# A planned graph-network kernel: own due times for every step, loads planned as a queue, a column of ones, split projections, and biases moved into ScalarE

## The chip, the cores and the metric

The kernel runs on one core of one Trainium2 chip. The metric is the device time of one execution in microseconds (us), the lower the better. The program that is launched is timed whole; the trace covers the span of its instructions.

## What is computed

Two layers run over 128 graphs (`B`) of 128 nodes, with 64 features per node. Both end in a residual sum and a layer norm.

```
mask = adj > 0
h    = relu((x @ W1a)[:, :, None] + (x[:, :, None] - x[:, None]) @ W1b + b1)   # 192 wide, per edge
hm   = einsum('bjkh,bjk->bjh', h, mask)
x1   = layernorm(x + hm @ W2 + deg * b2)
agg  = einsum('bmn,bnd->bmd', adj, x1)
h1   = elu(agg @ V1 + c1);  h2 = elu(h1 @ V2 + c2)                             # 128 wide
out  = layernorm(x1 + h2 @ V3 + c3)
```

About 6% of the entries of `mask` are one, so the kernel does not build all 128 x 128 edges of a graph: it sorts the nodes by degree, gives each sorted node a fixed number of edge slots (`BLOCKS`, 7 to 22), and handles only those 1323 slots per graph. A dense version stands behind a branch for graphs that do not fit; in the profiled execution it does not run.

## The kernel before

Graphs go in 64 pairs; the two graphs of a pair share the partitions where their data is 64 wide. One **round** is the work on one pair's worth of every step, though the steps of one round belong to different pairs: pair `p` is prepared some rounds before its edges are handled and finished some rounds after.

Each step is a Python generator that yields work items `(engine, cost, what it waits for, PSUM banks, function)`:

- `prepare` counts degrees (L511, VectorE), makes sort keys (L518-519, GpSimd), spreads them over the partitions (L524) together with a row of positions (L526, TensorE), ranks the nodes (L533) and makes a permutation matrix (L541, VectorE) that reads the row of positions from PSUM.
- `sort_x` and `project_a` sort `x` (L556) and compute the node term (L570 on TensorE, L577 on ScalarE adds `b1`); GpSimd and VectorE compute a correction for the unused slots (L584, L596, L603).
- `sort_mask` sorts the mask (L612, L615), forms prefix sums (L626) and nine one-hot tables (L636, VectorE).
- `turn` transposes the adjacency and `x` (L651, L652); `project_c` computes the neighbour term in float32 (L669), adds `b2` to its last 64 columns (L672) and splits it in three bfloat16 parts (L679, L683, L686, L688).
- `unit` is run nine times per pair, on four PSUM banks in turn: ScalarE writes the node term into a bank (L811), TensorE adds the gathered neighbour term with 18 matmuls in 64-column tiles (L823), VectorE sums absolute values over the slots (L832).
- `finish` subtracts the correction (L741), multiplies by `W2` (L746), adds the part from `project_c` (L750), counts degrees with two one-column matmuls against `mtp` (L753), undoes the sort (L763), normalizes (`norm`, L696 to L719), and runs layer 1: L770, hidden 1 (a bias row times ones, L778, then L780), `elu`, hidden 2 (a bias row times ones, L786, then L787), `elu`, last (L792, L794), `norm`, store.

In `elu`, the PSUM bank already holds z + 1 (the bias row carries c + 1): ScalarE takes exp(z) with a constant bias of -1 (L729), and VectorE takes max(z + 1, min(exp(z), 1)) (L732), reading one operand from PSUM and one from SBUF. The result is elu(z) + 1; the ones are taken out of the next layer's bias.

`Flow` sets the order of the work. It holds a clock per engine from the written costs, and at each turn takes, among the items that could start within `NEAR` (`NEAR_PE` for TensorE) of the earliest one on that engine, the one with the lowest due time. A change between 64-column tiles (`"PE:t"`) and the full array costs `SWITCH` and adds `HOLD` to the rank. `"PORT"` is a resource that a VectorE and a GpSimd item can both claim. Due times come from one formula: `ROUND * (p - AHEAD) + STEP * step`, with every later item of a thread `STEP` after the one before. The result is a fixed order of instructions on each engine; on the chip only semaphores hold it together, and the costs and the PORT play no part.

All loads are issued by SyncE. At the start, SyncE issues the loads of three pairs with `b1` and `b2` between them, then all constants of layer 1 (`arrive_late`), then the loads of later pairs (`load`, L498, L500). The planner assumes that a load lands 2.5 us after the engines' clock.

## Time and profile before

| what | value |
|---|---|
| median of 3 runs | 788.52 us (788.28 to 788.82) |
| profiled execution | 789.11 us, of which the trace's span is 787.3 us |
| TensorE matmul busy | 756.4 us, 96% of the span |
| VectorE busy | 736.8 us, 94% |
| ScalarE busy | 661.6 us, 84% |
| GpSimd busy | 441.7 us, 56% |
| mean granted TensorE clock | 0.991 |
| first edge unit on TensorE | 32.87 us after the span's start |
| last edge unit's matmuls begin | 763.91 us |

Busy time of an engine counts overlapping instructions once. A matmul's record includes its way through the array, so records of consecutive matmuls overlap; what one of them costs is read from its start to the start of the next. From 110 us on, the order of work repeats each round, and a round lasts 11.49 us.

### The profile page before, as it was taken

The page shows a single profiled execution, that of the slowest core. Times are in us where ns is not written, and L with a number is a line of the kernel's source. Part 1 is how long each engine was busy: PE and PEld are TensorE (multiplying, and loading weights), DVE is VectorE, ACT ScalarE, POOL GpSimd, SP SyncE. Part 2 cuts the span into 40 slices and gives each one's busy share as a digit, 9 for nine tenths or more (in the row PEclk, how much of TensorE's full clock was granted, in tenths as well). Part 3 has the DMA queues.
Part 4 walks back from the last instruction along what each step waited for, and adds up shares of the span by engine and source line. Part 5 has one row for each costly group of instructions (what it writes and reads, how often), then busy time and mean ns, then how long its engine had stood idle before and what let it go on. Part 6 is the DMA issues. An engine that isn't in the chain of part 4 may idle for free.

```text
span 787.3 us, 35836 instructions
## 1 busy us (share of the span) xinstructions
PE 756.4 (96%) x14551; PEld 684.9 (87%) x14552; DVE 736.8 (94%) x2421; ACT 661.6 (84%) x1862; POOL 441.7 (56%) x806
## 2 busy tenths in 40 slices
PE   4889999999999999999999999999999999999994
PEld 2578999999999999999999999999999999999983
DVE  3899999999999999999999999999999999999982
ACT  1868889898989989898998989889898988989862
POOL 4445556555655655565565556556556655655542
PEclk9999999999999999999999999999999999999996
DMA  3000101101101110110111011011101101110000
GB/s 95 2 2 23 27 22 27 30 20 30 26 20 30 27 29 20 30 27 20 30 27 29 21 30 26 20 30 26 30 20 31 26 20 30 27 28 21 9 9 14
DMA packets 63884, 19.91 MB, mean 25 GB/s; under 512 B 46560, under 2 KB 63712, under 8 KB 63712
## 3 DMA queue, kind: packets, MB, share of 16 engines
q1 hardware_dynamic: 63008, 17.25, 9.4%
q8 instruction: 116, 1.90, 1.0%
q14 instruction: 56, 0.46, 0.2%
q10 hardware_dynamic: 704, 0.30, 0.1%
HBM read 13.27 MB, written 4.19 MB: 22 GB/s over the span
## 4 chain that ended last, share of the span: by engine, by line
PE 91%; DVE 4%; ACT 1%; DMA 1%; issue 1%; SPq 1%; POOL 1%; ACTq 0%; POOLq 0%; DVEq 0%
PE e L823 43%; PE m L570 6%; PE m L746 6%; PE m L669 5%; PE m L780 4%; PE m L794 4%; PE m L787 4%; PE m L763 4%; PE m L770 2%; PE m L556 2%; PE m L651 2%; PE m L750 1%; PE m L672 1%; PE m L589 1%; DVE sums L832 1%; DVE oh L636 1%
## 5 line engine op out<-in xcount | busy, mean ns | idle before, releaser
L823 PE MATMUL e<-oh,cp 128*64 128x162 bf16 (+3 forms) x10368 | 376.4, 228 | 5.4 <-ACT e L811 3.8
L823 PEld LDWEIGHTS <-cp 128*64 128x64 bf16 x10368 | 349.1, 110 | 24.4 <-issue 16.9
L832 DVE TENSOR_REDUCE sums<-e 128x54 f32<-128x486 f32 (+8 forms) x576 | 345.6, 610 | 4.2 <-PE e L823 1.9
L811 ACT COPY e<-aj 128x504 f32<-128x504 f32 (+6 forms) x576 | 300.2, 549 | 17.0 <-DVE sums L832 11.6
L636 DVE TENSOR_TENSOR oh<-vp,slotc 128x336 bf16<-128x336 bf16 (+6 forms) x576 | 168.3, 321 | 0.7 <-PE e L823 0.5
L688 POOL TENSOR_TENSOR cp<-r,cp 128x512 bf16<-128x512 f32 x64 | 74.8, 1170 | 73.8 <-ACT cp L686 73.7
L709 POOL TENSOR_TENSOR rs<-ve,mhalf 128x2 f32<-128x2 f32 x128 | 89.2, 697 | 10.6
L577 ACT ACTIVATE aj<-m,b1c 128x128 f32<-128x128 f32 x192 | 56.5, 365 | 34.7 <-PE m L570 34.6
L741 POOL TENSOR_TENSOR hm<-sums,corr 128x384 f32<-128x384 f32 x64 | 64.3, 1004 | 31.1 <-DVE sums L832 31.1
L518 POOL CAST degb<-deg 128x2 bf16<-128x2 f32 x64 | 12.4, 193 | 122.5 <-DVE mk L511 122.5
L584 POOL TENSOR_TENSOR sa<-aj,srow 128x384 f32<-128x384 f32 x64 | 64.1, 1001 | 15.6 <-ACT xsT L560 8.3
L603 POOL TENSOR_TENSOR corr<-ea,sa 128x384 f32<-128x384 f32 x64 | 64.0, 1001 | 11.2 <-DVE ea L596 11.2
L679 ACT CAST cp<-m 128x256 bf16<-128x256 f32 x128 | 41.6, 376 | 33.3 <-PE m L672 33.2
L729 ACT ACTIVATE e<-m,mone 128x256 f32<-128x256 f32 x128 | 60.7, 474 | 6.7 <-PE m L787 3.7
L708 POOL TENSOR_SCALAR ve<-st 128x2 f32<-128x2 f32 x128 | 24.5, 191 | 67.1 <-DVE st L701 61.6
L732 DVE SCALAR_TENSOR_TENSOR h<-e,m 128x256 f32<-128x256 f32 x128 | 53.0, 414 | 5.5 <-ACT e L729 5.5
L570 PE MATMUL m<-xsT,wad 128*128 128x128 f32 x384 | 57.6, 287 | 0.5 <-DVE h L732 0.5
L746 PE MATMUL m<-w2d,hm 128*128 128x128 f32 x384 | 54.3, 278 | 0.0
L683 DVE TENSOR_TENSOR r<-m,cp 128x256 f32<-128x256 f32 x128 | 48.5, 419 | 5.8
L719 ACT ACTIVATE x<-y,nb,rs 128x64 f32<-128x64 f32 x128 | 51.1, 464 | 0.9 <-POOL nb L712 0.8
L570 PEld LDWEIGHTS m<-xsT,wad 128*128 128x128 f32 x384 | 48.7, 194 | 0.9 <-DVE h L732 0.7
L746 PEld LDWEIGHTS m<-w2d,hm 128*128 128x128 f32 x384 | 48.0, 192 | 1.1 <-POOL hm L741 0.2
(147 smaller groups left out, 1416.6 us busy)
## 6 DMA issues: line engine op xcount, KB each, us to landing
adj<-in_adj_dram SPq DMA_DIRECT2D x64, 128.0 KB, 2.4
xx<-in_x_dram SPq DMA_DIRECT2D x64, 64.0 KB, 2.1
out_dram<-o SPq DMA_DIRECT2D x64, 64.0 KB, 1.6
degs<-ys SPq DMA_DIRECT2D x64, 1.0 KB, 1.6
w1s<-in_L_gnn_W_dram ACTq DMA_DIRECT2D x2, 96.0 KB, 3.1
rows<-in_L_gnn_b_dram SPq DMA_DIRECT2D x3, 64.0 KB, 3.4
w2s<-in_L_gnn_W_dram ACTq DMA_DIRECT2D x2, 48.0 KB, 2.7
v2s<-in_L_gnn_W_dram SPq DMA_DIRECT2D x1, 64.0 KB, 2.3
```

The source lines that it names most:

```text
L570: nc.tensor.matmul(aps[:, c * N:(c + 1) * N], wad[:, c, :], xsT, start=True, stop=True)
L584: evs, = yield ("POOL PORT", 0.95, [have] + made("srow"), 0, lambda: nc.gpsimd.tensor_mul(sa, aj, srow))
L603: ev, = yield ("POOL PORT", 1.05, [ev, evs], 0, lambda: nc.gpsimd.tensor_sub(corr, ea, sa))
L636: lambda: nc.vector.tensor_tensor(oh[:, :, c].rearrange("p b (s w) -> p b s w", w=w), vp[:, :, p0:p1].rearrange("p b (o w) -> p b o w", o= ...
L688: lambda: nc.gpsimd.tensor_sub(cp[:, 2], r1, cp[:, 1]))
L709: nc.gpsimd.tensor_tensor(rs, ve, mhalf, op=OP.pow)
L729: lambda: nc.scalar.activation(e, z, AF.Exp, bias=mone))
L741: lambda: nc.gpsimd.tensor_sub(hm, d["sums"], d["corr"]))
L746: nc.tensor.matmul(yb[:, :2 * O], hm[:, c, :], flat(w2d[:, c]), start=(c == 0), stop=False)
L811: lambda: nc.scalar.copy(e.rearrange("p (c s w) -> p c s w", c=3, w=w), d["aj"][:, :, p0:p1].rearrange("p c (o w) -> p c o w", o=1) .to_br ...
L823: nc.tensor.matmul(e[s * HB:(s + 1) * HB, c * n:(c + 1) * n], cp[:, k, s, c * HB:(c + 1) * HB], oh[:, s, base:base + n], start=False, stop ...
L832: nc.vector.tensor_reduce(d["sums"][:, :, p0:p1], e.rearrange("p (c s w) -> p c w s", c=3, w=w), AX.X, OP.add, apply_absolute_value=True)
```

## The change

- **Due times.** The formula is replaced by a table `DUE` with one due time for each item of each thread, relative to the pair's round; `ROUND` goes from 11.39 to 10.88, and `NEAR`, `NEAR_PE` and `HOLD` change. `finish` reaches up to 67.86 us behind the round's start.
- **Loads' queue in the order.** A clock `SP` for SyncE's queue replaces the fixed landing times, and `arrive_late` is called after all threads have been started. In the built program the loads of a fourth pair now stand ahead of the constants of layer 1. `consts_slots` and `consts_more` become threads of their own.
- **Column of ones.** `wc` and `b2p` get two more columns, so that `project_c` makes 258 columns instead of 256, one of them constant 1; L750's matmuls are 65 wide and give the degrees, and L753's two matmuls go. L750's stand ahead of L746's.
- **C in turns.** The two float32 matmuls of `project_c` (256 columns each, one per graph) become four of 129 columns, alternating between the graphs.
- **Permutation row.** `permute` reads the positions from `iotb` (bfloat16, SBUF) and no longer from PSUM; L526's matmul goes.
- **Layer 1's biases.** The bias rows of hidden 1 and 2 go (L778, L786). ScalarE does relu(z + c) into a new tile `r` and exp(z + c), both with a bias column; VectorE takes min(r + 1, exp), both from SBUF. The PSUM bank is given back after ScalarE's second reading. The constant rows shrink from 384 to 128 columns.

In the built program a steady round has these groups on TensorE, in brackets those in 64-column tiles, by the names above. Before: [units of 112, 168, 154, 169 slots; L770, L556; 154, 170, 162, 66], L669, L672, L786, L787, L612, L615, [168], L589, L591, L778, L780, L746, L750, L753, L792, L794, L524, L526, L763, L570, L626, L651, L652. After: [170, 162, 66, 168; L770, L556; 112], L626, L792, L794, L787, L524, L750, L746, L570, L780, L651, L652, L763, [168, 154, 169, 154], L669, L672, L612, L615, L589, L591.

The diff, cut to its core (left out: where consts are made, the same edits in the dense version):

```diff
     LAG = 0.2
-    NEAR = 0.1
-    NEAR_PE = 0.05
+    NEAR = 0.05
+    NEAR_PE = 0.15
     SWITCH = 0.1
-    HOLD = 5
+    HOLD = 6.1
 
     def __init__(self, banks):
         self.clock = {}
...
         self.serial = 0
         self.mode = ""
 
-    def start(self, due, pace, gen):
+    def start(self, base, due, gen):
 
         self.serial += 1
-        th = [due, self.serial, pace, gen, None]
+        th = [0.0, self.serial, gen, iter(due), None, base]
         self._next(th, None)
 
     def _next(self, th, got):
         try:
-            th[4] = th[3].send(got)
+            th[4] = th[2].send(got)
         except StopIteration:
             if th in self.threads:
                 self.threads.remove(th)
             return
+        th[0] = th[5] + next(th[3], th[0] - th[5])
...
-    ROUND = 11.39
+    ROUND = 10.88
     AHEAD = 3
     PACE = ROUND / NB
-    STEP = 1.94
-    TURN = 4
-    CS = 3
-    SORT = 5
-    FIN = 0.5
-
-    def due(p, step):
-        return ROUND * (p - AHEAD) + STEP * step
+
+    DUE = {
+        "prepare": (-31.51, -35.16, -30.68, -28.51, -25.44),
+        "sort_x": (-21.45, -19.07, -15.96, -16.91, -9.73, -13.05, -11.84, -19.08, -7.31),
+        "sort_mask": (-25.43, -30.82, -14.74, -22.11, -22.67, -17.78, -15.78, -13.77, -11.69,
+                      -9.33, -20.75, -7.56, -14.87, -3.77),
+        "turn": (-24.58, -30.52),
+        "project_c": (-27.69, -27.43, -23.93, -20.73, -19.45, -14.51, -21.65),
+        "finish": (29.82, 26.25, 27.75, 29.86, 30.75, 40.45, 42.78, 44.15, 44.38, 49.48, 50.77,
+                   52.16, 51.8, 55.37, 57.47, 56.89, 62.45, 63.17, 67.86, 67.4, 65.33),
+        "unit": (-2.31, -0.69, 1.51),
+    }
 
     def pace(u):
         return PACE * u
 
+    def begin_thread(name, p, gen):
+        flow.start(ROUND * p, DUE[name], gen)
...
+    SP = [0.7]
+
+    def queued(cost):
+
+        SP[0] = max(SP[0], max(flow.clock.values(), default=0.0)) + cost
+        return [SP[0] + 2.6]
...
-    wc = const([P, H + O], F32, "wc")
+    wc = const([P, H + O + 2], F32, "wc")
...
-        happened([6.0], "const", "b1")
-        happened([6.0], "const", "b2")
+        happened(queued(1.4), "const", "b1")
+        happened(queued(0.5), "const", "b2")
 
     def arrive_late():
         fetch(v2s, g.v2)
         fetch(v3s, g.v3)
         for s in range(2):
             fetch(v1d[s * F:(s + 1) * F], g.v1)
-        for c, lo, times in ((g.c1, 0, 1), (g.c2, H1, 1), (g.c3, 2 * H1, 2)):
-            n = c.shape[0]
-            fetch(rows[:, lo:lo + times * n].rearrange("p (t n) -> p t n", t=times),
-                  bass.AP(tensor=c.tensor, offset=c.offset, ap=[[0, P], [0, times], [1, n]]))
-        happened([14.0], "const", "v")
-        happened([14.0], "const", "c")
+        for k, c in enumerate((g.c1, g.c2)):
+            fetch(cc[:, k:k + 1], c.rearrange("(h one) -> h one", one=1))
+        fetch(rows.rearrange("p (t n) -> p t n", t=2),
+              bass.AP(tensor=g.c3.tensor, offset=g.c3.offset, ap=[[0, P], [0, 2], [1, O]]))
+        happened(queued(2.2), "const", "v")
+        happened([queued(1.6)[0] + 3.0], "const", "c")
...
+        flow.start(0.1, [0.0], consts_prefix(below))
+        flow.start(DUE["sort_x"][0], [0.0], consts_slots())
...
+        yield from op("POOL", 0.2, lambda: v.memset(b2p, 0.0), "b2p0")
+        yield from op("POOL", 0.2, lambda: v.memset(b2p[0:1], 1.0), "b2p1")
...
-            nc.tensor.matmul(key[:, 2 * N:3 * N], small, iotb, start=True, stop=True)
-        ev, key = yield ("PE", 0.17, [ev] + made("identb", "small", "iotb"), 1, spread)
+        ev, key = yield ("PE", 0.11, [ev] + made("identb"), 1, spread)
...
         permb = d["permb"] = prep.tile([P, 2, N], BF16, name="permb")
 
         def permute():
             for s in range(2):
-                nc.vector.tensor_scalar(permb[:, s, :], key[:, 2 * N:3 * N], pos[:, s:s + 1], None,
+                nc.vector.tensor_scalar(permb[:, s, :], iotb, pos[:, s:s + 1], None,
                                         op0=OP.is_equal)
-        ev, = yield ("DVE", 0.51, [ev], 0, permute)
-        flow.give(key, ev)
-        flow.start(due(p, SORT), STEP, sort_x(p, ev))
-        flow.start(due(p, SORT), STEP, sort_mask(p, ev))
+        ev, = yield ("DVE PORT", 0.24, [ev] + made("iotb"), 0, permute)
+        begin_thread("sort_x", p, sort_x(p, ev))
+        begin_thread("sort_mask", p, sort_mask(p, ev))
...
-        cols = H + O
+        cols = H + O + 2
 
         def project(*cps):
-            for s in range(2):
-                k = slice(s * F, (s + 1) * F)
-                nc.tensor.matmul(cps[s][:, :cols], d["turned"][k, 2, :], wc[k, :],
-                                 start=True, stop=False)
+
+            half = cols // 2
+            for c in range(2):
+                for s in range(2):
+                    k = slice(s * F, (s + 1) * F)
+                    nc.tensor.matmul(cps[s][:, c * half:(c + 1) * half], d["turned"][k, 2, :],
+                                     wc[k, c * half:(c + 1) * half], start=(c == 0), stop=False)
             for s in range(2):
                 nc.tensor.matmul(cps[s][:, H:cols], onesb[:, :P], b2p, start=False, stop=True)
-        ev, *cps = yield ("PE", 0.7, [ev] + made("wc", "b2p", "onesb"), 2, project)
+        ev, *cps = yield ("PE", 0.6, [ev] + made("wc", "b2p", "onesb"), 2, project)
...
-    def elu(zb, ev, name):
+    def elu(zb, ev, name, k):
 
         z = zb[:, :2 * N]
+        c = cc[:, k:k + 1]
         e = work.tile([P, 2 * N], F32, name="e", bufs=5)
-        ev, = yield ("ACT", act(2 * N, 1), [ev], 0,
-                     lambda: nc.scalar.activation(e, z, AF.Exp, bias=mone))
+        r = work.tile([P, 2 * N], F32, name="r", bufs=3)
+        ev0, = yield ("ACT", act(2 * N, 1), [ev] + made("cc"), 0,
+                      lambda: nc.scalar.activation(r, z, AF.Relu, bias=c))
+        ev, = yield ("ACT", act(2 * N, 1), [ev] + made("cc"), 0,
+                     lambda: nc.scalar.activation(e, z, AF.Exp, bias=c))
+        flow.give(zb, ev)
         h = work.tile([P, 2 * N], F32, name=name)
-        ev, = yield ("DVE", dve(2 * N), [ev], 0,
-                     lambda: nc.vector.scalar_tensor_tensor(h, e, 1.0, z, op0=OP.min, op1=OP.max))
-        flow.give(zb, ev)
+        ev, = yield ("DVE PORT", dve(2 * N), [ev0, ev], 0,
+                     lambda: nc.vector.scalar_tensor_tensor(h, r, 1.0, e, op0=OP.add, op1=OP.min))
...
+        def cut(t):
+            return t[:, :2 * O + 4].rearrange("p (s o) -> p s o", s=2)[:, :, :O]
+
         def project(yb):
             cp, mtp = d["cp"], d["mtp"]
+
+            for s in range(2):
+                for i in range(3):
+                    nc.tensor.matmul(yb[:, s * (O + 1):(s + 1) * (O + 1)], mtp[:, s, :],
+                                     cp[:, i, s, H + 1 - s:H + 2 + O - s],
+                                     start=(s == 0 and i == 0), stop=False)
             for c in range(3):
-                nc.tensor.matmul(yb[:, :2 * O], hm[:, c, :], flat(w2d[:, c]),
-                                 start=(c == 0), stop=False)
-            for s in range(2):
-                for i in range(3):
-                    nc.tensor.matmul(yb[:, s * O:(s + 1) * O], mtp[:, s, :], cp[:, i, s, H:H + O],
-                                     start=False, stop=(s == 1 and i == 2))
-            for s in range(2):
-                nc.tensor.matmul(yb[:, 2 * O + s:2 * O + s + 1], mtp[:, s, :], onesb[:, 0:1],
-                                 start=True, stop=True)
-        ev, yb = yield ("PE", 0.9, [ev] + made("w2d"), 1, project)
-        ys = work.tile([P, 2 * O + 2], F32, name="ys")
-        ev, = yield ("ACT", act(2 * O + 2), [ev], 0, lambda: nc.scalar.copy(ys, yb[:, :2 * O + 2]))
+                nc.tensor.matmul(cut(yb), hm[:, c, :], w2d[:, c], start=False, stop=(c == 2))
+        ev, yb = yield ("PE", 0.8, [ev] + made("w2d"), 1, project)
+        ys = work.tile([P, 2 * O + 4], F32, name="ys")
+        ev, = yield ("ACT", act(2 * O + 2), [ev], 0, lambda: nc.scalar.copy(ys[:, :2 * O + 2], yb[:, :2 * O + 2]))
         flow.give(yb, ev)
-        nc.sync.dma_start(g.degs[:, 2 * p:2 * p + 2], ys[:, 2 * O:])
+        nc.sync.dma_start(g.degs[:, 2 * p:2 * p + 2], ys[:, O:O + 2])
 
         def unsort(t):
             for s in range(2):
                 nc.tensor.matmul(t[:, s * O:(s + 1) * O], d["permT"][:, s, :],
-                                 ys[:, s * O:(s + 1) * O], start=True, stop=True)
+                                 cut(ys)[:, s, :], start=True, stop=True)
...
         def hidden1(zb):
-            nc.tensor.matmul(zb[:, :2 * N], c1p, onesb, start=True, stop=False)
             for s in range(2):
                 nc.tensor.matmul(zb[:, s * N:(s + 1) * N], v1p[:, s, :], agg,
-                                 start=False, stop=(s == 1))
-        ev, zb = yield ("PE", 0.56, [ev] + made("v1p", "rowp"), 1, hidden1)
-        h1, ev = yield from elu(zb, ev, "h1")
+                                 start=True, stop=True)
+        ev, zb = yield ("PE", 0.45, [ev] + made("v1p"), 1, hidden1)
+        h1, ev = yield from elu(zb, ev, "h1", 0)
 
         def hidden2(zb):
-            nc.tensor.matmul(zb[:, :2 * N], c2p, onesb, start=True, stop=False)
-            nc.tensor.matmul(zb[:, :2 * N], v2s, h1, start=False, stop=True)
-        ev, zb = yield ("PE", 0.55, [ev], 1, hidden2)
-        h2, ev = yield from elu(zb, ev, "h2")
+            nc.tensor.matmul(zb[:, :2 * N], v2s, h1, start=True, stop=True)
+        ev, zb = yield ("PE", 0.44, [ev], 1, hidden2)
+        h2, ev = yield from elu(zb, ev, "h2", 1)
...
-            happened([max(flow.clock.values(), default=1.0 + p) + 2.5], "load", p)
-            flow.start(due(p, 0), STEP, prepare(p))
-            flow.start(due(p, TURN), STEP, turn(p))
+            happened(queued(1.0), "load", p)
+            begin_thread("prepare", p, prepare(p))
+            begin_thread("turn", p, turn(p))
...
+    flow.start(-97.0, [0.0], consts_wad())
+    flow.start(DUE["sort_x"][2], [0.0], consts_b2())
+    flow.start(-95.0, [0.0], consts_banks())
+    flow.start(ROUND * -0.5, [0.0], consts_late())
+    for k in range(NE):
+        flow.start(pace(k), DUE["unit"], lane(k, [0.0]))
     arrive_late()
```

## The prediction, made before the change was run

> **What bounds the kernel now.** I read the busy shares and the chain first, then stages, then one round of TensorE in order of time.
>
> ```profile
> PE 756.4 (96%) x14551; PEld 684.9 (87%) x14552; DVE 736.8 (94%) x2421; ACT 661.6 (84%) x1862; POOL 441.7 (56%) x806
> ...
> PE 91%; DVE 4%; ACT 1%; DMA 1%; issue 1%; SPq 1%; POOL 1%; ACTq 0%; POOLq 0%; DVEq 0%
> ```
>
> The chain that ended last runs through TensorE for 91% of the span. The stages (us, then busy time of TensorE, its weight loads, VectorE, ScalarE, GpSimd):
>
> ```profile
> 0.00:32.87 32.87, 19.92 (x117) 12.94 (x118) 17.34 (x93) 14.11 (x43) 12.55 (x50) 1.00 0.23 58
> 32.87:110.05 77.18, 71.62 (x1394) 63.56 (x1395) 74.56 (x235) 61.66 (x168) 41.74 (x67) 1.00 0.07 16
> ...
> 764.70:787.30 22.60, 10.70 (x63) 7.26 (x61) 5.87 (x19) 6.24 (x18) 6.38 (x15) 0.67 0.06 13
> ```
> ```profile
> 282.45:293.94 11.49, 11.49 (x229) 10.55 (x231) 11.27 (x38) 10.23 (x30) 6.76 (x13) 1.00 0.12 27
> ```
>
> A steady round (last fence) is 11.49 us, TensorE without a gap, VectorE at 98%, ScalarE at 89%. So the price of a TensorE instruction is what it adds to that row, and every other engine has little to give. Idle TensorE time: 13.0 us ahead of the first unit, 5.6 in the ramp, 11.9 at the tail. One round on TensorE, start of each group first:
>
> ```profile
> 161.10 0.70 PE L669 MATMUL m<-wc,turned 64*128 64x256 f32 x4
> 161.74 0.23 PE L672 MATMUL m<-b2p,onesb 128*128 128x64 bf16 x2
> 161.80 0.27 PE L786 MATMUL m<-onesb,rowp 128*128 128x256 bf16 x1
> 161.91 0.60 PE L787 MATMUL m<-h,v2s 128*128 128x256 f32 x2
> ...
> 163.63 0.27 PE L778 MATMUL m<-onesb,rowp 128*128 128x256 bf16 x1
> 163.74 0.61 PE L780 MATMUL m<-agg,v1p 128*128 128x128 f32 x4
> ...
> 165.03 0.19 PE L753 MATMUL m<-onesb,mtp 128*128 128x1 bf16 x2
> 165.08 0.22 PE L792 MATMUL m<-rowp,onesb 128*128 128x128 bf16 x1
> ...
> 165.69 0.22 PE L526 MATMUL m<-iotb,small 128*128 128x128 bf16 x1
> 165.75 0.61 PE L763 MATMUL m<-ys,permT 128*128 128x64 f32 x4
> 166.19 0.89 PE L570 MATMUL m<-xsT,wad 128*128 128x128 f32 x6
> 166.92 0.27 PE L626 MATMUL m<-mtp,prefix 128*128 128x256 bf16 x1
> ```
>
> The difference of two starts is what a group costs. At the head one wait stands out (waited for: us, times, longest), and its cause in SyncE's queue, in its order of time:
>
> ```profile
> PE m L651 <- DMA adj<-in_adj_dram: 8.5, 2, 7.1
> ```
> ```profile
> 8.53 1.53 SPq L236 DMA_DIRECT2D rows<-in_L_gnn_b_dram  x3
> 10.11 0.47 SPq L498 DMA_DIRECT2D adj<-in_adj_dram  x1
> ```
>
> The fourth pair's adjacency is issued at 10.11, behind the constants, and lands at 16.1; its transpose stands in TensorE's order ahead of the first pair's sort keys, so from 9.13 to 16.24 TensorE does nothing and the first pair waits with it.
>
> **What the Trainium skill says.** (1) "TensorEngine Tiling (Array Packing)", Key Properties: tiles work in parallel, a change of tiling mode drains the array. The trace agrees: L669's two graphs run side by side, and a change costs about 0.1 us (L652's matmul takes 0.20 us ahead of a tiled unit, where 0.11 would be its share of L651's). (2) "SBUF — State Buffer", Who interferes with whom: a VectorE instruction with two SBUF inputs holds up, or is held up by, a GpSimd instruction that reads SBUF; `tensor_scalar` in a two-port mode excludes GpSimd altogether. The one-hot L636 takes 235 to 1240 ns here, so this exists. (3) "ScalarE: Activation LUTs", Table sets: relu lies in exp's set, so no table load is added; the trace has one load, and the program of after has one too. (4) "VectorE: DVE Perf Modes", The perf-mode tier table: `tensor_scalar` on bfloat16 in SBUF may run four elements a cycle, PSUM operands may not.
>
> **The change, part by part (us per round).**
>
> *Rows out of TensorE:* L786 161.91-161.80 = 0.11; L778 163.74-163.63 = 0.11; L753 165.08-165.03 = 0.05; L526 165.75-165.69 = 0.06. Sum -0.33, all on the path. Bounds 0.30 to 0.36: a following float32 load could have hidden part.
>
> *Order on TensorE:* as many mode changes as before (four a round, and one entry into L669's row tiles). L763 (64-column float32) now ends a group. L570 after it cost 166.92-166.19 = 0.73 for six matmuls, where six of L746 cost 0.67; after L746 it should cost 0.67 (-0.06). L652 with its full stream and drain gives way to L763 with 53 ns less to stream (-0.05). L746 comes after short bfloat16 matmuls, so its first weight load is seen (+0.03). Sum -0.08, bounds -0.15 to +0.05.
>
> *C in turns:* now 161.74-161.10 = 0.64. Columns rise only from 256 to 258; the pairs ran side by side already, so I see nothing that alternation adds. Eight shorter streams instead of four put float32 weight loads (0.11 us each, L763's spacing) beside streams of equal length: +0.02. The trace has no such form: bounds -0.10 (the load seen at the start, or the drain, goes) to +0.20 (loads not hidden). The 65th and 66th column add under 0.01.
>
> TensorE: 11.49 - 0.33 - 0.08 + 0.02 = 11.10.
>
> *Permutation from SBUF:* two L541 start 0.25 apart; the one like instruction from SBUF, L377, lasts 214 ns against 338. Two times 0.12 off VectorE: -0.24. `elu` on VectorE, 414 ns, has as many elements: 0. VectorE: 11.27 - 0.24 = 11.03.
>
> *Relu on ScalarE:* two more instructions like L729 (474 ns, the next one starting 0.37 later): +0.74. ScalarE: 10.23 + 0.74 = 10.97. Each relu stands on ScalarE's queue ahead of its exp and of the following copies for units (L811), for which TensorE waits if they are late; four banks filled ahead hide that, and if they were not, each would cost 0.37.
>
> So three engines need 11.10, 11.03 and 10.97. VectorE's gaps before were 0.22 and can't all vanish; I let a round last 11.15, with 11.05 (all slots fit) and 11.35 (gaps stay, and one PORT wait of some 0.1) as ends. Gain 64 x 0.34 = 21.8 us.
>
> *Head:* the fourth load is issued in fourth place, about 6.4 (where v2s was), and by the 2.4 us to landing of the page, or the 6.0 seen here, lands at 8.8 to 12.4. Before, the first pair's L612 ran at 20.1. Now its keys still wait for GpSimd's one-hot constants (to 6.4 before), then ranks follow product and copy of `wc` (cold, until 9.0): L612 at about 11. From L612 to the first unit was 12.8 us; with fewer pairs prepared in between (L669 of the first pair now right behind its L570) about 10. First unit near 21 instead of 32.9, but 1.5 to 2 us of preparation are still to be done: -10, bounds -5 to -13. The constants of layer 1 come about 1 us later; the first hidden 1 is far behind.
>
> *Tail:* two relus of 0.37 stand in the last pair's serial chain (+0.7), and more unfinished pairs crowd it (about 10.7 us of TensorE work behind the last unit, about 6 before), which also takes work out of the rounds ahead: +1.5, bounds -2 to +4. degs stores and outputs move with their steps; SyncE's queue has slack (mean 25 GB/s).
>
> Sum on the span: 787.3 - 21.8 - 10 + 1.5 = 757.0. The profiled execution took 789.11, its span 787.3; the median of the runs, 788.52, is 1.2 over that span. So 758.2.
>
> **Rivals.**
>
> *A, TensorE gains more.* Alternation saves the 0.10, and the order fits: round 10.99 (VectorE then has to close up, 11.03 against it: some gaps shrink). 787.3 - 32 - 10 + 1.5 + 1.2 = 748. For it: VectorE's and ScalarE's busy times contain overlaps of their own. Against: nothing in the trace shows where L669 would get faster.
>
> *B, VectorE or ScalarE takes over.* Round 11.35: 787.3 - 9 - 10 + 1.5 + 1.2 = 771. For it: VectorE was at 98% with TensorE as the only brake, ScalarE goes from 89% to 98%. Against: its work per round is still below TensorE's.
>
> *C, the port, slower.* The two new L732 read both operands from SBUF, and GpSimd spends about 4.2 us a round in L584, L603, L741, L688 (1.0 to 1.17 us each). No semaphore keeps them apart. If one of VectorE's new port users a round begins behind one of these, it stands for up to 1.0 us, and everything behind it on VectorE, the sums of the units first. From 0.61 us a round on (11.49 - 11.03 + 10/64) the kernel is slower; at 1.0 the round is 12.13 and the time 787.3 + 41 - 10 + 1.5 + 1.2 = 821. Against: one-hots, with the same need, run at 321 ns in the mean.
>
> *D, the head doesn't do what it says:* the load still lands late, DMA being 42% busy there: -4 instead of -10, about 764. It lies in the forecast's own range.
>
> **Chances.** Forecast with D (749 to 767) 0.56; A (740 to 749) 0.17; B (767 to 784) 0.19; C 0.06; the rest, within 0.2% (about what a measurement of this kernel can tell from no change), 0.02. Faster 0.92, same 0.02, slower 0.06. The range takes most of A and half of B: 744 to 774.
>
> **What would show it.** Round in the stages: 11.15, TensorE without gaps; if VectorE has none and TensorE some, B. L669's group 0.65; 0.54 is A. L541 near 214 ns. L732 long or its start late after GpSimd: C. First unit near 21 us and no wait for adjacency over 3 us at L651. I'm wrong if the round's groups, other than those removed, cost more than their starts show now.

## The result, and the profile after

The changed kernel takes 798.16 us (median of 4 runs, 797.01 to 800.29) against 788.67 for the kernel before: 1.0124 times the time, 95% interval 1.0100 to 1.0148. Measured once more, beside some of the experiments, it took 798.67 against 789.38: 1.0105 (1.0087 to 1.0123). The forecast was 758.2. The profiled execution took 800.29 us, its span is 797.4, against 789.11 and 787.3 before.

Busy shares of after:

```profile
PE 753.9 (95%) x14487; PEld 689.9 (87%) x14488; DVE 757.4 (95%) x2422; ACT 713.6 (89%) x1990; POOL 468.5 (59%) x807
```

TensorE has a little less to do than before (753.9 for 756.4), VectorE 20.6 us more (757.4 for 736.8), although an operation was meant to become shorter there. The stages of after; the columns are those of the stages in the prediction (length, then busy time of TensorE, its weight loads, VectorE, ScalarE, GpSimd): the head up to the first unit, and the tail from the last matmul of a unit on; then one steady round.

```profile
0.00:20.87 20.87, 15.24 (x103) 11.42 (x104) 14.31 (x81) 12.17 (x36) 13.49 (x51) 0.95 0.35 85
...
769.41:797.40 27.99, 17.69 (x116) 13.68 (x111) 10.45 (x34) 13.82 (x43) 10.77 (x25) 0.69 0.09 18
```
```profile
405.25:417.13 11.88, 11.47 (x232) 10.59 (x229) 11.72 (x39) 11.08 (x32) 7.25 (x13) 1.00 0.10 24
```

The tail of before, cut at the same event:

```profile
764.53:787.30 22.77, 10.87 (x69) 7.30 (x63) 6.04 (x20) 6.24 (x18) 6.38 (x15) 0.68 0.06 13
```

The head is 12.0 us shorter (32.87 before). The tail is 5.2 longer. Between them lie 748.5 us where 731.7 were: +16.9. The sum, -12.0 + 16.9 + 5.2 = +10.1, is the difference of the spans. So the head gave what was forecast, and the rounds, which should have given 22, took 17. In the round TensorE now has 0.41 us without work, VectorE 0.16. Which of VectorE's instructions grew is read from the groups by shape (line, engine, operation, output and inputs, count, then busy us and mean ns of one):

```profile
L661 DVE TENSOR_TENSOR oh<-vp,slotc 128x224 bf16<-128x224 bf16 x64 | 62.0, 969 | 0.0
L765 DVE SCALAR_TENSOR_TENSOR h<-r,e 128x256 f32<-128x256 f32 x128 | 53.9, 422 | 4.9 <-ACT e L761 4.9
...
L661 DVE TENSOR_TENSOR oh<-vp,slotc 128x336 bf16<-128x336 bf16 x128 | 41.8, 327 | 0.0
...
L567 DVE TENSOR_SCALAR permb<-iotb,pos 128x128 bf16<-128x128 bf16 x128 | 26.3, 245 | 0.0
```

The first of these shapes in the kernel before:

```profile
L636 DVE TENSOR_TENSOR oh<-vp,slotc 128x224 bf16<-128x224 bf16 x64 | 19.9, 311 | 0.0
```

One shape of the one-hots, that of 112 slots (2 x 112 = 224 elements), takes 969 ns; a larger one with 336 takes 327, and before, this one took 311 in the mean. 55 of the 576 one-hots last over 700 ns in after, 4 in the kernel before. The two operations that the change did touch on VectorE, the new `elu` (L765, 422 for 414) and the permutation (L567, 245 for 338), are near their forecasts (414 and 214). What stands beside the long one-hot is seen in the order of time (start in us, length, engine, line; here and in the like fences below VectorE and GpSimd alone):

```profile
407.61 1.00 POOL L609 TENSOR_TENSOR sa<-aj,srow 128x384 f32<-128x384 f32 x1 [1.15 <-ACT aj L602]
...
408.95 0.55 DVE L621 SCALAR_TENSOR_TENSOR ea<-aj,m 128x384 f32<-128x384 f32 x1
409.43 0.42 DVE L765 SCALAR_TENSOR_TENSOR h<-r,e 128x256 f32<-128x256 f32 x1
409.65 1.05 POOL L628 TENSOR_TENSOR corr<-ea,sa 128x384 f32<-128x384 f32 x1 [1.04 <-DVE ea L621]
409.76 1.09 DVE L661 TENSOR_TENSOR oh<-vp,slotc 128x224 bf16<-128x224 bf16 x1
410.77 0.67 DVE L863 TENSOR_REDUCE sums<-e 128x51 f32<-128x510 f32 x1
```

`ea` on VectorE releases `corr` on GpSimd. Two places behind `ea` on VectorE stands the one-hot, with both operands in SBUF. `corr` comes in while `h` is at work, and the one-hot ends at 410.85, just after `corr` has ended at 410.70. Nothing in the program makes it wait: the only semaphore that this one-hot waits for is TensorE's. A record's start doesn't show the wait either: the length does. In the kernel before, the same one-hot began 0.13 us after `corr` had ended (418.50 + 1.00 = 419.50):

```profile
418.50 1.00 POOL L603 TENSOR_TENSOR corr<-ea,sa 128x384 f32<-128x384 f32 x1
...
419.43 0.29 DVE L696 TENSOR_TENSOR y<-m,xx 128x128 f32<-128x128 f32 x1
419.63 0.28 DVE L636 TENSOR_TENSOR oh<-vp,slotc 128x224 bf16<-128x224 bf16 x1
```

In after, the sum behind the one-hot, then `r` (L711), come later by the same amount, and for `r` TensorE waits, once in each of 55 rounds (waited for: total us, times, longest):

```profile
PE m L581 <- DVE r L711: 22.4, 55, 0.4
```

Read from start to start the loss is larger than these 0.4 us: the group ahead of this wait (L803) takes 0.78 us to the start of L581, and 0.22 in the kernel below whose one-hot was moved; L581 takes 0.27 for 0.22. That is 0.61 of the 0.66 us by which a round of after is longer than one of that kernel.

### The profile page after: what moved, and what is told of

The parts are those of the page before. It is cut to its first block, busy times and chain, and to the rows that moved or that the text cites. A ratio compares the mean times of both kernels' runs of the same rounds, so it can differ in the third digit from the quotient of the medians.

```text
span 797.4 us, 35842 instructions
## 1 busy us (share of the span) xinstructions
PE 753.9 (95%) x14487; PEld 689.9 (87%) x14488; DVE 757.4 (95%) x2422; ACT 713.6 (89%) x1990; POOL 468.5 (59%) x807
## 5 line engine op out<-in xcount | busy, mean ns | idle before, releaser
L842 ACT COPY e<-aj 128x504 f32<-128x504 f32 (+6 forms) x576 | 304.4, 550 | 47.7 <-DVE sums L863 45.2
L661 DVE TENSOR_TENSOR oh<-vp,slotc 128x336 bf16<-128x336 bf16 (+6 forms) x576 | 208.1, 388 | 3.2 <-PE e L854 3.2
L716 POOL TENSOR_TENSOR cp<-r,cp 128x516 bf16<-128x516 f32 x64 | 78.6, 1228 | 54.1 <-ACT cp L714 52.0
L737 POOL TENSOR_TENSOR rs<-ve,mhalf 128x2 f32<-128x2 f32 x128 | 94.4, 737 | 10.7
L759 ACT ACTIVATE r<-m,cc 128x256 f32<-128x256 f32 x128 | 60.8, 475 | 4.6 <-PE m L818 2.8
L761 ACT ACTIVATE e<-m,cc 128x256 f32<-128x256 f32 x128 | 61.2, 478 | 0.0
L765 DVE SCALAR_TENSOR_TENSOR h<-r,e 128x256 f32<-128x256 f32 x128 | 53.9, 422 | 4.9 <-ACT e L761 4.9
L787 PE MATMUL m<-w2d,hm 128*128 128x128 f32 x384 | 58.3, 288 | 0.0
L711 DVE TENSOR_TENSOR r<-m,cp 128x258 f32<-128x258 f32 x128 | 52.5, 412 | 2.5 <-ACT cp L707 2.5
L707 ACT CAST cp<-m 128x258 bf16<-128x258 f32 x128 | 48.5, 385 | 0.7 <-PE m L700 0.7
L581 PE MATMUL m<-permf,xx 128*64 128x128 f32 x256 | 27.9, 296 | 22.4 <-DVE r L711 22.4
L787 PEld LDWEIGHTS m<-w2d,hm 128*128 128x128 f32 x384 | 47.8, 191 | 0.0
```

What stands on the lines that cost most here:

```text
L661: lambda: nc.vector.tensor_tensor(oh[:, :, c].rearrange("p b (s w) -> p b s w", w=w), vp[:, :, p0:p1].rearrange("p b (o w) -> p b o w", o= ...
L716: lambda: nc.gpsimd.tensor_sub(cp[:, 2], r1, cp[:, 1]))
L737: nc.gpsimd.tensor_tensor(rs, ve, mhalf, op=OP.pow)
L761: lambda: nc.scalar.activation(e, z, AF.Exp, bias=c))
L787: nc.tensor.matmul(cut(yb), hm[:, c, :], w2d[:, c], start=False, stop=(c == 2))
L842: lambda: nc.scalar.copy(e.rearrange("p (c s w) -> p c s w", c=3, w=w), d["aj"][:, :, p0:p1].rearrange("p c (o w) -> p c o w", o=1) .to_br ...
```

## The experiments

**The theories.** T: in each round the one-hot stands at the SBUF port that VectorE and GpSimd share, behind `corr`, for 1.09 - 0.31 = 0.78 us. Without that, a round would take what TensorE's groups add up to, about 11.2. R1: VectorE and ScalarE are simply full, and the wait takes time that would be lost anyway. R2: it isn't GpSimd's reading that matters, any GpSimd instruction bars the one-hot. R3: a one-hot that is moved only meets `sa` in place of `corr`. R4: it needs what only after has (the new `elu`, the new planner). The ratios are to the kernel before, run on the same chip:

| kernel | us | ratio (95%) | one-hot of 112 slots, ns | round, us |
|---|---|---|---|---|
| after, beside the last ones | 798.67 | 1.0105 (1.0087-1.0123) | 969 in the first profile | 11.88 |
| one-hot moved ahead of `ea` | 762.39 | 0.9651 (0.9635-0.9667) | 291 | 11.22 |
| `corr` cut | 759.59 | 0.9612 (0.9596-0.9628) | 286 | 11.22 |
| memsets for `corr` | 760.30 | 0.9619 (0.9603-0.9635) | 287 | 11.22 |
| memsets on `ea` | 760.51 | 0.9631 (0.9615-0.9647) | 286 | 11.22 |
| before, one-hot moved behind `corr` | 823.59 | 1.0429 (1.0411-1.0446) | 766 | 12.11 |
| before, loads' order alone | 782.61 | 0.9901 (0.9885-0.9918) | 311 | 11.49 |
| one-hot moved, two rows back | 771.72 | 0.9776 (0.9758-0.9794) | 293 | 11.39 |
| one-hot moved, `elu` behind a sum | 772.08 | 0.9780 (0.9763-0.9796) | 291 | 11.40 |
| one-hot moved, statistics ahead of `elu` | 763.94 | 0.9679 (0.9663-0.9695) | 291 | 11.22 |
| other plan, no port for `elu` | 784.28 | 0.9924 (0.9906-0.9943) | 282 | 11.54 |
| other plan, relu into PSUM | 791.54 | 1.0028 (1.0020-1.0036) | 286 | irregular |

**The one-hot moved** (after; VectorE's order changed by one instruction: `ea` puts out the pair's fourth one-hot, that of 112 slots, ahead of itself, and the one-hot's own turn then does nothing):

```
+        def mask():
+            d.pop("early", lambda: None)()
+            nc.vector.scalar_tensor_tensor(
...
+        ev, = yield ("DVE", dve(3 * N), [ev], 0, mask)
...
+            if i == 3:
+                d["early"] = onehot
+                onehot = lambda: d.pop("early", lambda: None)()
```

> The changed kernel with one instruction moved: in each round the one-hot of 112 slots is issued on VectorE just ahead of `ea` instead of two places behind it; every other instruction keeps its place. Theory T (the one-hot stands at the shared port behind GpSimd's `corr`, which `ea` releases; 0.78 us a round): the one-hot falls from 969 to about 310 ns, the steady round from 11.89 to 11.1 to 11.25 (TensorE's groups add up to 11.2), the time to about 798 - 64 x 0.68 = 755 (749 to 762). Rival R1 (VectorE or ScalarE is full and the plan's order leaves no slack; the stall only takes time that would be lost anyway): the one-hot falls, the round stays above 11.7 and the time above 786. Rival R3 (the one-hot now meets GpSimd's `sa`, which runs just before): the wait moves, the one-hot stays near 900 ns, the time near 798.

Measured 762.39 us, a little over T's 749 to 762; R1 and R3 are out. One steady round of this kernel, and the same place in it:

```profile
409.11:420.33 11.22, 11.22 (x229) 10.58 (x228) 10.96 (x38) 11.00 (x32) 7.07 (x13) 1.00 0.12 26
```
```profile
412.70 0.53 DVE L663 TENSOR_TENSOR oh<-vp,slotc 128x336 bf16<-128x336 bf16 x2
413.17 0.55 DVE L622 SCALAR_TENSOR_TENSOR ea<-aj,m 128x384 f32<-128x384 f32 x1
413.64 0.42 DVE L771 SCALAR_TENSOR_TENSOR h<-r,e 128x256 f32<-128x256 f32 x1
413.87 1.05 POOL L630 TENSOR_TENSOR corr<-ea,sa 128x384 f32<-128x384 f32 x1 [1.04 <-DVE ea L622]
413.97 0.68 DVE L869 TENSOR_REDUCE sums<-e 128x51 f32<-128x510 f32 x1
```

Two one-hots (x2) now take 0.53 together, ahead of `ea`; behind `h` comes a sum, which reads PSUM and goes on beside `corr`. TensorE has no gap (11.22 of 11.22). So after loses 36 us, from 798.7 to 762.4, through the place of one instruction of 0.3 us.

**`corr` cut** (after, order untouched; also, `hm` takes `sa` in place of `corr`, so `sa` gets eight buffers instead of three; the masked maximum is left out of the correction in this run and in the two with memsets):

```
-        corr = d["corr"] = prep.tile([P, 3, N], F32, name="corr", bufs=7)
+        corr = prep.tile([P, 3, 1], F32, name="corr", bufs=7)
+        d["corr"] = sa
...
-    nc.gpsimd.tensor_sub(corr, ea, sa)
+    nc.gpsimd.tensor_sub(corr, ea[:, :, :1], sa[:, :, :1])
```

> The changed kernel, its order untouched, but `corr` on GpSimd is cut from 3 x 128 columns to 3 x 1, and `hm` takes `sa` in its place; so the masked maximum is left out of the correction. T: nothing to stand behind, the one-hot of 112 slots at about 310 ns, round 11.1 to 11.25, time about 755 (749 to 762), like the run with the one-hot moved. R1: round above 11.7, time above 786.

759.59 us, round 11.22, one-hot 286 ns: with its old place but nothing to stand behind, it doesn't stand. That both ways end at the same 11.22 suggests that this is TensorE's need and no longer VectorE's; the run with two rows back, below, shows it.

**Memsets for `corr`:**

```
+            nc.gpsimd.tensor_sub(corr[:, :1], ea[:, 0, :1], sa[:, 0, :1])
+            for _ in range(2):
+                nc.gpsimd.memset(corr, 0.0)
```

> As the run with `corr` cut, but GpSimd is kept as long as before at the same place by instructions that only write: one column subtracted, then two memsets of 448 columns (about 0.15 + 2 x 0.43 = 1.0 us by the 194 ns of a memset of 128 columns). The masked maximum is left out of the correction here too. T in its narrow form (it is GpSimd's reading that bars the one-hot, as the Trainium skill has it in SBUF - State Buffer, Who interferes with whom): the one-hot stays near 310 ns, time about 755. Rival R2 (any GpSimd instruction on SBUF bars it, reading or not): the one-hot waits as before for 0.7 to 0.9 us, time 790 to 800.

760.30 us. It looks like an answer and isn't one: in the order of time the one-hot starts at 412.68, beside the short subtraction (412.57 to 412.81), and the first memset only at 412.87. Hence the next.

**Memsets on `ea` itself** (after; `corr` replaced):

```
-    nc.gpsimd.tensor_sub(corr, ea, sa)
+            for _ in range(2):
+                nc.gpsimd.memset(ea, 0.0)
```

> The changed kernel, its order untouched, with `corr` replaced by two memsets of `ea` itself (3 x 128 columns each, about 0.4 us by the 471 ns of one of 448 columns), released by `ea` as `corr` is; GpSimd so only writes at the place where the one-hot of 112 slots starts (in the earlier run with memsets the one-hot had slipped in ahead of the first of them, so it did not decide). The masked maximum is left out of the correction. If reading is what bars the one-hot: its row at 290 to 330 ns, time 755 to 763. If any GpSimd access to SBUF does: the row at 600 ns or more, time over 775.

760.51 us, row 286 ns. In the order of time:

```profile
412.42 0.42 DVE L768 SCALAR_TENSOR_TENSOR h<-r,e 128x256 f32<-128x256 f32 x1
412.56 0.90 POOL L630 MEMSET ea<- 128x384 f32 x2 [0.95 <-DVE ea L621]
412.75 0.29 DVE L664 TENSOR_TENSOR oh<-vp,slotc 128x224 bf16<-128x224 bf16 x1
412.95 0.68 DVE L866 TENSOR_REDUCE sums<-e 128x51 f32<-128x510 f32 x1
```

GpSimd is at work from 412.56 to 413.46, and the one-hot ends at 413.04 at its usual length. A GpSimd operation that only writes doesn't bar it, one that reads does. That agrees with the Trainium skill ("SBUF — State Buffer", Who interferes with whom), and R2 is out for these operations.

**The kernel before with the one-hot moved behind `corr`** (before; the reverse experiment: `EARLY` holds the one-hot of 112 slots that is due three places later):

```
         def add():
             nc.vector.tensor_add(flat(y), yps[:, :2 * O], flat(rest))
+            if not shift and EARLY:
+                EARLY.pop(min(EARLY))()
```

> The kernel BEFORE with nothing of the change in it and one instruction moved on VectorE: the one-hot of 112 slots is issued three places earlier, right behind the second layer norm's first sum, about 0.3 us after GpSimd has begun `corr` (9.52 to 10.52 in a round counted from the permutation; the one-hot would be due at about 9.9). T (where the one-hot stands in relation to a GpSimd operation that reads is all it takes): it waits about 0.6 to 0.7 us, VectorE needs 11.27 + 0.65 = 11.9 us a round against 11.49, the time rises by about 64 x 0.42 = 27 us to 816 (808 to 824), and its row shows over 800 ns instead of 311. Rival R4 (what makes after slow needs something that only after has: `elu` from two SBUF operands, the new planner): one-hot near 311 ns, time within 1% of before.

823.59 us, 1.0429 of before; the upper end of T's 808 to 824. R4 is out: nothing of the change is in it. Its group, and a round's place:

```profile
L637 DVE TENSOR_TENSOR oh<-vp,slotc 128x224 bf16<-128x224 bf16 x64 | 49.0, 766 | 0.0
```
```profile
412.03 1.00 POOL L604 TENSOR_TENSOR corr<-ea,sa 128x384 f32<-128x384 f32 x1
412.15 0.29 DVE L701 TENSOR_TENSOR y<-m,x 128x128 f32<-128x128 f32 x1
412.36 0.82 DVE L637 TENSOR_TENSOR oh<-vp,slotc 128x224 bf16<-128x224 bf16 x1
413.10 0.33 DVE L534 SCALAR_TENSOR_TENSOR cmp<-m,keyc,tie 128x128 bf16<-128x128 f32 x1
```

The wait here is 0.82 - 0.29 = 0.53 us, which takes VectorE's 11.27 to 11.80; the round grows by 0.62, to 12.11. TensorE loses all of this at one place: from start to start, the group ahead of L656 takes 0.67 us instead of 0.11 and L656 itself 0.27 instead of 0.22, since L656 waits for a `y` of VectorE that comes late. Why this is 0.09 more than the one-hot's own wait is open. `y`, which takes one operand from PSUM, runs beside `corr` at its usual 0.29.

**Loads' order alone** (before; the late constants behind the fourth pair's load):

```
             arrive_next()
-    arrive_late()
...
+    arrive_late()
     flow.run()
```

> The kernel before with one part of the change alone: the late constants are loaded after the fourth pair instead of ahead of it. If the head's gain is a gain of the whole (the prediction's -10 with the work that has to be done later), the first unit starts near 22 instead of 32.9 us and the time is 776 to 782, with the round at 11.49 as before. If what is not prepared in the head only comes back in the ramp, the time stays within 786 to 789.

782.61 us, just above the expected 776 to 782. The first unit starts at 27.05, not near 22: of the 12 us that the head gained in after, the load's place alone makes 5.8. TensorE still waits 2.6 us for one adjacency here, and in after for none. In after fewer steps of other pairs stand ahead of the first unit, by the new due times; I didn't try those alone, so where the rest comes from is not shown. The gain is kept to the end (-7.3 by the medians), with the round at 11.49.

**Two rows back** (on the kernel with the one-hot moved; the rows are zeros and add nothing):

```
+            nc.tensor.matmul(zb[:, :2 * N], zero, onesb, start=True, stop=False)
             for s in range(2):
                 nc.tensor.matmul(zb[:, s * N:(s + 1) * N], v1p[:, s, :], agg,
-                                 start=True, stop=True)
+                                 start=False, stop=(s == 1))
```

(and the same ahead of `v2s, h1`.)

> The kernel with the one-hot moved, plus two matmuls a round that add nothing: a bf16 row of 128 x 256 of zeros into each hidden layer, where the bias rows stood before (L786 and L778, 0.11 us each by the prediction). If TensorE sets the round once the wait at the port is gone (11.22, no gap), the round becomes 11.22 + 0.22 = 11.44 and the time 762.4 + 64 x 0.22 = 776 (774 to 779). If ScalarE (98%) or VectorE (98%) sets it, or the rows hide beside float32 weight loads, less than half of that: 762 to 769.

771.72 us, between the two ranges: +9.3 instead of +14, round +0.165 instead of +0.22. TensorE has no gap here either. On TensorE in the order of time:

```profile
410.05 0.61 PE L834 MATMUL m<-v3s,h 128*128 128x64 f32 x4
410.50 0.27 PE L826 MATMUL m<-onesb,zero 128*128 128x256 bf16 x1
410.61 0.60 PE L827 MATMUL m<-h,v2s 128*128 128x256 f32 x2
411.04 0.28 PE L551 MATMUL m<-identb,degb 128*128 128x128 bf16 x2
...
412.76 0.27 PE L818 MATMUL m<-onesb,zero 128*128 128x256 bf16 x1
412.87 0.61 PE L820 MATMUL m<-agg,v1p 128*128 128x128 f32 x4
```

With the row, `h,v2s` takes 411.04 - 410.61 = 0.43 from start to start. Without it, in the kernel with the one-hot moved, the same group takes 0.488 in the mean of 32 rounds. So the row of 0.11 buys back 0.054: behind it the float32 group is shorter (perhaps its weight load is hidden; that isn't shown). The row ahead of `agg,v1p` costs its full 0.109, since that group took 0.447 with and without. 0.109 + 0.109 - 0.054 = 0.164 is the whole growth of the round: what is added on TensorE is what the round grows by, so TensorE does set it.

**`elu` behind a sum, and statistics ahead of `elu`** (both on the kernel with the one-hot moved). First the exchange of `h` with the sum behind it (`EA` is set by `ea`, and the next sum puts out what is in `WAIT`):

```
+            if EA:
+                EA.clear()
+                WAIT.append(least)
+            else:
+                least()
```

> The kernel with the one-hot moved, and the new `elu` operation that followed `ea` on VectorE exchanged with the sum behind it: it is now issued about 0.65 us after `ea`, while GpSimd's `corr` (1.05 us, begun 0.2 us after `ea`) is running. Rival C as the prediction put it (any operation with two SBUF operands stands there, the new `elu` too): one of two `elu` operations a round waits 0.4 to 0.6 us, the mean of its row goes from 426 to 600 to 730 ns, VectorE needs 10.95 + 0.5 = 11.45, the time 775 to 785. Theory T2 (what stands is the bfloat16 operations in a faster mode: one-hots and, in the run with the other plan, the permutation, which was 1086 ns at its worst place; the float32 operations [...] share the port and don't stand): the row stays under 460 ns, the time at 760 to 765.

772.08 us, the `elu` row at 507 ns: under the 600 of rival C and over the 460 of T2. The order of time decides where the numbers didn't:

```profile
407.68 1.01 POOL L636 TENSOR_TENSOR corr<-ea,sa 128x384 f32<-128x384 f32 x1 [1.04 <-DVE ea L627]
407.76 0.69 DVE L885 TENSOR_REDUCE sums<-e 128x51 f32<-128x510 f32 x1 [0.23 <-PE e L876]
408.37 0.60 DVE L777 SCALAR_TENSOR_TENSOR h<-r,e 128x256 f32<-128x256 f32 x1
408.64 1.18 POOL L793 TENSOR_TENSOR hm<-sums,corr 128x384 f32<-128x384 f32 x1
```

`corr` ends at 408.69, and `h` at 408.97, 0.60 after its start where the other `elu` of the round takes 0.41. It waited only 0.2 because little of `corr` was left, and the round grew by 0.18. So the new `elu`, float32 with two SBUF operands, stands there too: T2 falls. Then the attempt at a longer wait:

```
                 op0=OP.max, op1=OP.mult)
+            nc.vector.bn_stats(junk, ident)
```

> The kernel with the one-hot moved, plus one statistics instruction on VectorE that nothing uses (128 columns, about 0.22 us), right behind `ea`: the new `elu` operation behind it now falls due just after GpSimd has begun `corr`, with 0.8 us of it still to go, where the exchange with a sum had left it 0.25. Rival C (float32 with two SBUF operands stands there too): the `elu` row, two a round, goes from 426 ns to 750 to 900 in the mean, the round to 11.22 + 0.6 to 0.8 = 11.8 to 12.0, the time to 800 to 812. If it shares the port and only slows a little: row under 500 ns, time 762 to 768 (VectorE 10.95 + 0.22 = 11.17, still under 11.22).

763.94 us, `elu` row 421 ns: the timing missed by 0.02 us, and it shows the other side.

```profile
415.37 0.41 DVE L773 SCALAR_TENSOR_TENSOR h<-r,e 128x256 f32<-128x256 f32 x1
415.39 1.26 POOL L632 TENSOR_TENSOR corr<-ea,sa 128x384 f32<-128x384 f32 x1 [1.05 <-DVE ea L623]
```

`h` came first, and now `corr` is the one that waits: 1.26 us, where it takes 1.00 beside no such operation. GpSimd has time, so the round stays at 11.22. The statistics instruction, 0.22 more on VectorE, is absorbed as well: VectorE had that much to spare.

**Two other plans.** In the first the planner no longer counts `elu` as a user of the port:

```
-        ev, = yield ("DVE PORT", dve(2 * N), [ev0, ev], 0,
+        ev, = yield ("DVE", dve(2 * N), [ev0, ev], 0,
```

> The changed kernel with one word changed in its plan: the planner no longer counts the new `elu` operation on VectorE as a user of the port, so it lays out another order on every engine; the instructions are the same. In that order `ea` is followed by two subtractions from PSUM and the mask, and the next one-hot starts about 1.2 us after `ea`, when `corr` (1.05 us) is about over. T: no one-hot over 450 ns in the mean, round 11.1 to 11.35, time 755 to 770. R (it was `elu` that suffers or does harm at the port): its row rises over 500 ns and the time stays above 785.

784.28 us. The one-hots are as short as T says (282 ns), and the time isn't. The reason is neither T's nor R's: another operation stands there.

```profile
412.53 1.25 DVE L567 TENSOR_SCALAR permb<-iotb,pos 128x128 bf16<-128x128 bf16 x2
412.54 1.03 POOL L609 TENSOR_TENSOR sa<-aj,srow 128x384 f32<-128x384 f32 x1 [0.67 <-ACT aj L602]
```
```profile
L567 DVE TENSOR_SCALAR permb<-iotb,pos 128x128 bf16<-128x128 bf16 x128 | 64.3, 544 | 0.0
```

The permutation, which the change moved from PSUM into SBUF, now meets `sa`: two of them take 1.25 us instead of 0.39, and VectorE is at work for 11.58 of 11.58 us of a round. It has one SBUF operand only; that a `tensor_scalar` on bfloat16 can still be shut out is what the skill says in the same section (VectorE's two-port modes), and this trace agrees. The 93 ns that the move saves per instruction are so bought with a new risk. That this alone makes the plan slow isn't shown: the order of everything changed with it. In the second plan relu goes in place into PSUM:

```
-                      lambda: nc.scalar.activation(r, z, AF.Relu, bias=c))
+                      lambda: nc.scalar.activation(e, z, AF.Exp, bias=c))
...
+                     lambda: nc.scalar.activation(z, z, AF.Relu, bias=c))
```

> The changed kernel with relu written in place into PSUM behind exp, so that the new VectorE operation reads one operand from PSUM and one from SBUF and needs no port, and its bank is given back after it; the plan comes out in another order. T: time 757 to 772 if the order leaves no one-hot behind a GpSimd operation, which it doesn't by its places (`ea` is followed by sums and ranks for over 1.2 us). Against it: banks are held about 0.8 us longer twice a round, which could leave TensorE without one (waits of TensorE for `h` or banks over 10 us in all): 775 to 790.

791.54 us, over both expectations. One round is not like the next. In five of them two one-hots in a row stand behind `corr` and `sa` (16 one-hots over 500 ns in all). VectorE and ScalarE are not full (105.3 and 103.6 of 111 us); TensorE nearly is (109.9), and its single waits for `h` add up to 6 us, not over 10. So its groups cost more: over 22 rounds the units come in 3.9 stretches a round, 3 in the kernel with the one-hot moved, and take 5.74 us a round from start to start instead of 5.50. What lengthens them stays open. It says nothing on relu from PSUM by itself, since the order of everything changed.

## Why the prediction was wrong, point by point

**The failed step is VectorE's sum, "11.27 - 0.24 = 11.03".** It priced VectorE's instructions at their durations of before and let only the touched ones change. The one-hots were untouched, but the new due times put one of them behind an operation that releases `corr`. That added 0.78 us, and 11.03 + 0.78 = 11.81 is about the round that came, 11.88. Without it the step is right to 0.07: 10.96 in the kernel with the one-hot moved. (The permutation saved 0.19 a round, not 0.24: it takes 245 ns, not 214.)

**Rival C had the mechanism, the price and the threshold** ("From 0.61 us a round on"), and 0.06 as its chance. By that threshold 0.78 had to make the kernel slower, and it did. (Its 12.13 for a wait of 1.0 is 0.1 more than its own 11.03 + 1.0; the threshold doesn't have this 0.1.) Two things in it were off. It looked for the victim among the *new* users of the port, and the victim was an old one. And its argument against, "one-hots, with the same need, run at 321 ns in the mean", is the error proper: that mean belonged to before's order, in which only 4 of 576 lasted over 700 ns. Moving one of them by three places in before made it 766 ns and the kernel 4.3% slower. The mean told nothing of a plan in which all places change. The orders of both kernels could have been laid side by side for just this: which operation with two SBUF operands comes next but one behind the instruction that releases a long GpSimd operation.

**TensorE, forecast 11.10, needs 11.22** (the round of five kernels in the table). The rows: -0.28 for -0.33, since a row in L786's place, put back into the order of after, cost 0.055 and not 0.11; that is just outside the prediction's bounds (0.30 to 0.36), which had expected something of the kind. C in turns: 0.722 for 0.702 before, +0.02 as forecast; alternation gains nothing, so rival A's reason falls. The order: what is left, 11.22 - 11.49 + 0.28 - 0.02 = about -0.01 for -0.08, inside its bounds. Two of its three parts came as forecast: L570 -0.053, and L763 in L652's place -0.053. The third, the product of `hm` and `w2d`, costs 0.747 from start to start where L746 cost 0.670: +0.08 and not +0.03.

**ScalarE, forecast 10.97:** 11.00 in the kernel with the one-hot moved, relu 475 ns as its nearest row said. TensorE waits for none of its copies in a steady round of that kernel. Right.

**Head, forecast -10:** -12.0, first unit at 20.87 for "near 21". The size is near, the cause half shown: the load's place alone gave 5.8.

**Tail, forecast +1.5 within -2 to +4:** +5.2, and +3.9 with the one-hot moved. Behind the last unit TensorE is now busy for 17.7 us, before for 10.9 (the step had about 10.7 and about 6; the 6 doesn't fit the 10.70 in its own line): more unfinished pairs, as the step said, but more than it took. This work is missing in the rounds ahead, which I take to be part of why the 55 waiting rounds (55 x 0.39 = 21) lengthen the middle by only 16.9. I made no run for the tail, so its division between relu and crowding is open.

**The rest of the sum.** With the one-hot moved the time is 762.4, 27.5 below before on its chip, where the forecast had 30.3 less. Part of this nearness is luck: on the spans the head gave -12.5 for -10, the middle -19.6 for -21.8, the tail +3.9 for +1.5, and the first error makes up for one of the others. That kernel beats both.

## What to carry to other kernels

A duration in a profile holds for the order in which it was taken: where VectorE and GpSimd share a port, list for each long GpSimd operation that reads SBUF which VectorE instruction releases it and what stands one and two places behind. If that has two SBUF operands, or is a bfloat16 `tensor_scalar` like the permutation, price it at what is left of the GpSimd operation, up to the whole of it. A planner that counts the port keeps such a pair apart only in its own time: here both the one-hot and `corr` were counted as its users, and on the chip, with no semaphore between them, they met. What reads PSUM can stand in that place: the sum (0.68 us beside `corr`) and `y` (0.29) ran there at their usual lengths.

## What the runs showed of the hardware

- The wait lasts to the other operation's end and goes both ways: the one-hot took 1.09 us instead of 0.31 behind `corr` and ended 0.15 us after it, in before with the one-hot moved too (413.18 after 413.03); `corr` took 1.26 instead of 1.00 behind `h`, which had started 0.02 us ahead of it.
- A `tensor_scalar` with one bfloat16 operand in SBUF stood for a whole `sa` (two in 1.25 us instead of 0.39). The masks (float32, with an accumulator, L537) hardly felt GpSimd: in the plan with relu in PSUM they took 281 ns (median) beside `hm`, 283 beside `sa`, and 279 beside nothing.
- A matmul of 256 bfloat16 columns ahead of a float32 group cost 0.055 us in one place and 0.109 in another: a price taken from the difference of two starts is that of its place.
